# Choosing experts in smaller groups of tiles near the end of layers 0 and 2, and handing out scatters without a limit in the last steps of layer 2

## The chip, the cores and the metric

The kernel runs on one core of a Trainium2 chip. The metric is the time of one execution on the device, in microseconds (us); lower is better. The core has a matrix engine (TensorE, PE in the profile), a vector engine (VectorE, DVE), a scalar engine (ScalarE, ACT), a general engine (GpSimd, POOL) and a sync engine (SyncE, SP) that here only issues DMA transfers. Each works through its own queue in order; they wait for each other by semaphores. GpSimd also issues the indirect DMA transfers, here called scatters: 128 rows are written to 128 places in DRAM that a column of integer indices gives.

## The reference, cut to what matters

8192 tokens of 128 numbers pass through four layers, each a cross attention with 16 heads and then a feed-forward part. The feed-forward parts of layers 0, 2 and 3 are mixtures of 8 experts. Layers 0 and 2 are the ones that the change touches:

```python
# layer 0: one expert for each token, at most T / E = 1024 tokens for an expert
logits = xf @ W_sw + b_sw;  probs = softmax(logits)
routes = argmax(probs);     onehot = one_hot(routes, E)
pos = cumsum(onehot, axis=0) - 1          # place within the expert, in order of the tokens
keep = pos_tok < capacity
buf[routes, pos_safe] = xs;  expert_out = gelu(buf @ W1 + b1) @ W2 + b2
final = where(keep, expert_out[routes, pos_tok], xs)

# layer 2: the two best experts for each token, no capacity
weights, indices = top_k(softmax(x @ router), 2)
norm_weights = softmax(weights)
out = sum over the two experts e of norm_weight_e * (silu(x @ G[e]) * (x @ U[e])) @ D[e]
```

The place of a token within its expert counts all tokens before it, so groups of tokens are placed one after the other.

## The kernel before

**Tiles and groups.** The tokens are 64 tiles of 128 and stay in `x_sb` in SBUF for the whole run, 132 columns a token (128 numbers and four for the routing). While a layer's attention is still running, the experts of the tiles that are finished are chosen, group by group, and their rows are scattered to a table in DRAM (`slots`), sorted by expert. The experts' part then reads the table tile by tile. It can only begin when the last scatter has landed: every read (`xe`) waits for all scatters.

**What choosing consists of.** For a group: `variance` (seven small VectorE operations, L238 to L244), `root` (two on ScalarE, L248 and L250), `norms` (four on VectorE, L255 to L258 and L1531), `tokens` (normalised rows `fxn`: on GpSimd, L1118, in layer 0, and on ScalarE, L1552, in layer 2, where GpSimd also copies the group's rows to `rec`, L1548, since each row goes to two places), `turn` (four transposes `prt` on TensorE, L1562, and a copy `rT` on ScalarE, L1564), `logits` (four pairs of matmuls `plg`, L1571, and a move on VectorE), `offs` and `exps` (a maximum, a subtraction, an exponential), `best` (VectorE: some 19 operations in layer 2, L1600 to L1635, and six in layer 0, L1132 to L1154, that end with `took` and `before`), `gates` (layer 2) and `places` (two matmuls `pup` on TensorE, L1167 and L1168 or L1654 and L1655, and VectorE's indices: `fc_r` at L1178 in layer 0, `pl_i` at L1668 in layer 2). `places` puts one scatter for each tile (layer 0) or two (layer 2) in the list `ready`; `scatter(n)` (L1679) issues at most n of them, all from line L1683. In layer 2, `tables` (L1704) computes from the final counts which expert each tile of the table belongs to.

**Order.** A plan says in which step of the attention each of these parts is issued. TensorE's order is written by hand (`manual_schedule`) in layer 0; in layer 2 TensorE's, ScalarE's and VectorE's are. On GpSimd the scheduler may move things, but `after_scatters` (L1698) makes the first GpSimd operation that comes after some scatters in the program wait for their issue, and later scatters wait for it, so these keep the program's order.

**Layer 0** (`wide_steps`, L317) has a step for each tile, i = 0 to 64; `scatter(2)` closes every step, and what the plan has left after step 64 follows with `scatter(16)`. The groups are 16, 16, 16, 8, 4 and 4 tiles. Counted from the step at which its last tile is done, a group of 16 has its `places` nine steps on, a group of 8 six, and a group of 4 three; with 4 tiles, `logits`, `best` and `places` are all in that third step.

**Layer 2** (`head_steps`, L589, with `layer == 2`) has a step n for each two tiles, n = 0 to 31, and then up to 39 without heads; each step has two halves, h = 2n and 2n + 1, in which the plan's parts and then a `scatter` are issued: at most 3 in the first half and 2 in the second while n is below 32, later 16 and 2. Within a step TensorE's order is: the maxima of step n + 1 (`sa`), the values of step n - 1 (`pav`), a piece of a later projection, the output of step n - 2 (`py`, L992), the parts of h = 2n, the scores of step n (`sb`), `po` of step n - 1, another piece, the parts of h = 2n + 1, and a transpose of the maxima (`pm`). In every odd n, the first piece is `head_tokens` (L730): GpSimd normalises four tiles (`xn`, L741) and adds a bias to them (L748), and TensorE at once transposes the four `xn` (`pxn`, L756). The last such call is in n = 27, for tiles 60 to 63. The groups are six of 8 tiles (0 to 47) and four of 4. After a group's last tile e, `places` comes at h = e + 13 for a group of 8 that ends with tile e, at e + 10 for a group of 4, and at e + 7 for the last one, which has a shorter plan and then `tables`. So tiles 32 to 39 are placed at h = 52, tiles 40 to 47 at 60, 48 to 51 at 61, 52 to 55 at 65, 56 to 59 at 69, and 60 to 63 at 70.

Of the kernel before, what the change touches and what calls it, by code (L numbers as in the profile page):

```python
# [41 lines left out]
class Net:  # L42
# [546 lines left out]
    def head_steps(self, layer, w, NH):  # L589


        proj, mT, aT, raw, o = {}, {}, {}, {}, {}
        self.ctxT = {}
        self.context(0)

        def piece(n, late):

            g, step = (n // 2 + 1, n % 2) if layer == 3 else ((n + 3) // 2, (n + 1) % 2)
            if 4 * g >= self.NT:
                return  # L600
            if g not in proj:
                proj[g] = {}
                self.head_tokens(g, layer, w, proj[g])
            step = 2 * step + late
            if layer == 3:
                step = (0, 2, 1, 3)[step]
                if step == 1 and 4 * g + 4 < self.NT:

                    proj[g + 1] = {}
                    self.head_tokens(g + 1, layer, w, proj[g + 1])  # L610
            if step == 0:
                if layer == 2:
                    self.head_mask_read(g, proj[g])
                self.head_transpose(g, proj[g])
            elif step == 1:
                if layer == 2:
                    self.head_mask(g, proj[g])
                self.head_queries(g, w, proj[g])
            elif step == 2:
                if layer == 2:  # L620
                    self.head_mask_T(g, proj[g])
                self.head_keys(g, w, proj[g])
            else:
                self.head_new_values(g, w, proj[g])

        proj[0] = {}
        outputs = {}
        if layer != 2:
            outputs = self.outputs_plan(layer)
            for step in sorted(outputs):  # L630
                if step[0] < (-2 if layer == 3 else 0):
                    for do in outputs.pop(step):
                        do()
        self.head_tokens(0, layer, w, proj[0])
        self.head_keys(0, w, proj[0])
        self.head_new_values(0, w, proj[0])
        if layer == 2:
            self.head_mask_read(0, proj[0])
            self.head_mask(0, proj[0])
            self.head_mask_T(0, proj[0])  # L640
        self.head_transpose(0, proj[0])
        self.head_queries(0, w, proj[0])
        if layer == 3:

            first = self.first_plan(3)
            for n in range(-2, NH + 8):
                for do in outputs.pop((n, 0), ()):
                    do()  # L650
                new, old, older = (0 <= m < NH for m in (n, n - 1, n - 2))
                if new:
                    st = self.head_stable(n, proj[n // 2])
                    self.head_stable_exp(st, 0)
                if old:
                    raw = self.head_values(n - 1, aT.pop(n - 1))
                if new:
                    self.head_stable_sum(st, 0)
                    self.head_stable_exp(st, 1)
                if older:  # L660
                    oT = self.head_turn(o.pop(n - 2))
                if new:
                    piece(n, False)
                    self.head_stable_sum(st, 1)
                for do in first.pop(2 * n, ()):
                    do()
                self.scatter(2 if n < NH else 16)
                if old:
                    o[n - 1] = self.head_back(layer, raw)
                if new:  # L670
                    self.head_stable_exp(st, 2)
                if older:
                    self.head_output(n - 2, layer, w, oT)
                    if n % 2 == 1:
                        self.first_fill(2 * n - 6)
                if new:
                    self.head_stable_exp(st, 3)
                    self.head_stable_sum(st, 2)
                    piece(n, True)
                for do in first.pop(2 * n + 1, ()):  # L680
                    do()
                self.scatter(2)
                if new:
                    self.head_stable_sum(st, 3)
                    aT[n] = st["aT"]
                for do in outputs.pop((n, 1), ()):
                    do()
            return
        piece(-1, False)
        piece(-1, True)  # L690
        mT[0] = self.head_maxima_T(0, self.head_maxima(0, proj[0]))
        choice = self.choice_plan() if layer == 2 else {}
        scatter = self.scatter if layer == 2 else lambda n: None
        for n in range(NH + 8):
            for do in outputs.pop((n, 0), ()):
                do()
            if n + 1 < NH:
                mx = self.head_maxima(n + 1, proj[(n + 1) // 2])
            if 0 <= n - 1 < NH:
                raw[n - 1] = self.head_values(n - 1, aT.pop(n - 1))  # L700
            if n < NH:
                piece(n, False)
            if 0 <= n - 2 < NH:
                self.head_output(n - 2, layer, w, o.pop(n - 2))
            for do in choice.pop(2 * n, ()):
                do()
            scatter(3 if n < NH else 16)
            if n < NH:
                aT[n] = self.head_softmax(n, proj[n // 2], mT.pop(n))
            if 0 <= n - 1 < NH:  # L710
                o[n - 1] = self.head_back(layer, raw.pop(n - 1))
            if n < NH:
                piece(n, True)
            for do in choice.pop(2 * n + 1, ()):
                do()
            scatter(2)
            if n + 1 < NH:
                mT[n + 1] = self.head_maxima_T(n + 1, mx)
            if 0 <= n - 1 < NH and layer != 2:
                o[n - 1] = self.head_turn(o[n - 1])  # L720
            for do in outputs.pop((n, 1), ()):
                do()
# [331 lines left out]
    def first_plan(self, layer):  # L1054
# [3 lines left out]
        norms, tokens, turn, logits = self.choice_norms, self.first_tokens, self.choice_turn, self.choice_logits  # L1058
        offs, exps, best, places = self.choice_offs, self.choice_exps, self.first_choose, self.first_places
        at = lambda f, t0: lambda g: f(g, t0)  # L1060
        if layer == 0:
            sizes = [16] * (self.NT // 16 - 1) + [8, 4, 4]
            plans = {
                16: [
                    (1, [variance, root]), (2, [norms, at(tokens, 0), at(tokens, 4)]),
# [38 lines left out]
        plan, i0 = {}, 0  # L1104
# [354 lines left out]
    def choice_constants_from(self, whole):  # L1459

        nc, const = self.nc, self.const
        self.groups = [(i, 8) for i in range(0, self.NT - 16, 8)]
        self.groups += [(i, 4) for i in range(self.NT - 16, self.NT, 4)]
        self.go_on = {}
        for n in (4, 8, 16):
            t = const.tile([P, E, n + 1], F32, name=f"go_on{n}")
            nc.gpsimd.memset(t, 1.0)
            nc.gpsimd.memset(t[:, :, 0:1], 0.0)
            self.go_on[n] = t
        ej = whole.tile([P, E], I32, name="ej")  # L1470
        nc.gpsimd.iota(ej, pattern=[[self.T, E]], base=0, channel_multiplier=0)
        self.expert_row = const.tile([P, E], F32, name="expert_row")
        nc.vector.tensor_copy(self.expert_row, ej)
        self.last_row = const.tile([P, E], F32, name="last_row")
        nc.vector.tensor_scalar_add(self.last_row, self.expert_row, -1.0)
        jj = whole.tile([1, self.NJ], I32, name="jj")
        nc.gpsimd.iota(jj, pattern=[[1, self.NJ]], base=0, channel_multiplier=0)
        self.tile_no = const.tile([1, self.NJ], F32, name="tile_no")
        nc.vector.tensor_copy(self.tile_no, jj)
# [13 lines left out]
    def choice_plan(self):  # L1493
# [18 lines left out]
            ],  # L1512
            [
                (0, [variance, root, norms]), (1, [at(tokens, 0), at(turn, 0)]),
                (2, [at(logits, 0), offs, exps]), (3, [best]), (4, [gates, places, tables]),
            ],
        ]
        plan, last = {}, len(self.groups) - 4
        for k, (i0, n) in enumerate(self.groups):
            g = {"i": i0, "n": n, "xT": {}, "xn": {}}  # L1520
            for when, calls in ends[k == last + 3] if k >= last else long:
                when += 2 * ((i0 + n) // 2 + 1)
                plan.setdefault(when, []).extend([(lambda f=f, g=g: f(g)) for f in calls])
        return plan

    def norms_to_rows(self, g):
# [486 lines left out]
```

## Time and profile before

| | us |
|---|---|
| median of 9 runs (lowest, highest) | 2697.72 (2691.32, 2703.39) |
| the profiled execution | 2692.33 |
| its span on the core | 2690.6 |

Where the span goes, by stretches (busy time of each engine in us, and the mean TensorE clock that was granted, 1.00 being full speed):

| stretch (us from the start) | length | PE | DVE | ACT | POOL | PE clock |
|---|---|---|---|---|---|---|
| 0 to 815: layer 0, attention and choosing | 815 | 743 | 411 | 380 | 241 | 0.98 |
| 815 to 965: layer 0, experts | 150 | 125 | 35 | 56 | 70 | 0.90 |
| 965 to 1270: layer 1, attention | 305 | 259 | 201 | 157 | 55 | 0.92 |
| 1270 to 1485: layer 1, feed-forward | 215 | 111 | 177 | 150 | 131 | 0.71 |
| 1485 to 1905: layer 2, attention and choosing | 420 | 363 | 235 | 192 | 161 | 0.92 |
| 1905 to 2150: end of choosing, layer 2, experts | 245 | 206 | 159 | 145 | 159 | 0.90 |
| 2150 to 2510: layer 3, attention | 360 | 254 | 292 | 241 | 167 | 0.84 |
| 2510 to 2690: layer 3, experts | 180 | 136 | 58 | 56 | 81 | 0.86 |

The table is read by rows: an engine whose busy time is close to the length sets the pace there. The change lies at the end of the first and around the boundary of the fifth and sixth stretch. A line of a timeline has the start, the length, engine, line, operation, output and inputs, and in brackets how long the engine sat idle before it and who ended that; a merged line stands for several instructions (x4). A scatter's line shows its time on GpSimd, not the transfer.

### The profile page before, as it was taken

To read this page: it belongs to the slowest core of one execution; us is meant where nothing else is said; L and a number is where in the kernel's file an instruction comes from. 1 tells how busy PE (TensorE), PEld (TensorE's weight loads), DVE (VectorE), ACT (ScalarE), POOL (GpSimd) and SP (SyncE) were. 2 spreads that over 40 slices of the span, in tenths; PEclk is the share of its full clock that TensorE was granted. 3 is DMA by queue.
4 is the path that set the end of the run, shared out by engine and by line. 5 is a ranking of instruction groups with operands and counts; after the bars stand their busy time and mean duration, and the time that the engine had idled before them with its cause. 6 is when DMAs were issued, how large, how long until landed. Compare 5 with 4: busy or idle time off the path is not lost.

```text
span 2690.6 us, 75308 instructions
## 1 busy us (share of the span) xinstructions
PE 2196.7 (82%) x31578; PEld 1693.9 (63%) x31578; DVE 1568.7 (58%) x4342; ACT 1376.4 (51%) x2712; POOL 1063.7 (40%) x1307
## 2 busy tenths in 40 slices
PE   5999999999987968996546898988399867777597
PEld 4777777777765746775324575666299845555465
DVE  5555454554542256656887565555577668888432
ACT  3444444444433425563777454444277547777232
POOL 2222243232343551111665305533666672344444
PEclk9999999999997969998677898999599968888599
DMA  9994000000002140000000101110133450111121
GB/s 254 271 245 101 10 24 24 12 20 22 16 24 71 41 144 15 22 19 13 0 1 1 25 16 38 37 31 27 59 90 90 130 153 25 42 35 40 49 61 43
DMA packets 215363, 157.41 MB, mean 59 GB/s; under 512 B 27237, under 2 KB 191984, under 8 KB 215025
## 3 DMA queue, kind: packets, MB, share of 16 engines
q1 hardware_dynamic: 193744, 117.22, 16.9%
q0 software_dynamic: 16640, 32.22, 3.6%
q8 instruction: 250, 4.10, 0.6%
q10 hardware_dynamic: 4640, 3.15, 0.4%
q14 instruction: 89, 0.72, 0.1%
HBM read 68.62 MB, written 86.31 MB: 58 GB/s over the span
## 4 chain that ended last, share of the span: by engine, by line
PE 55%; DVE 17%; ACT 9%; POOL 9%; issue 5%; DMA 5%; SPq 0%; DVEq 0%; POOLq 0%; ACTq 0%
PE pqk L391 9%; PE ph L1817 4%; PE py L487 4%; PE pv L413 4%; PE po L473 3%; POOL slots L1683 3%; PE py L1838 2%; PE sb L879 2%; PE pav L937 2%; PE ph L1231 2%; PE sc L429 2%; PE pt L457 2%; PE pye L1250 2%; PE sb L886 2%; ACT low L920 2%
## 5 line engine op out<-in xcount | busy, mean ns | idle before, releaser
L446 POOL TENSOR_TENSOR a<-a,sm 128x1024 f32<-128x1024 f32 x64 | 121.7, 1901 | 448.6 <-DVE sm L445 231.7
L891 ACT ACTIVATE aT<-sb 128x512 f32<-128x512 f32 x256 | 132.1, 603 | 181.6 <-PE sb L886 181.6
L852 DVE TENSOR_REDUCE mpad<-sa 128x8 f32<-128x512 f32 x256 | 158.9, 683 | 95.7 <-PE sa L847 95.6
L492 DVE TENSOR_TENSOR x_sb<-x_sb,py 128x128 f32<-128x128 f32 x64 | 18.4, 288 | 287.7 <-PE py L487 287.7
L460 ACT COPY aT<-pt 128x512 f32<-128x512 f32 x128 | 68.8, 589 | 207.2 <-PE pt L457 207.2
L1683 POOL DMA_INDIRECT slots<-x_sb,fc_r x128 | 124.8, 975 | 100.1 <-DVE fc_r L1178 50.7
L1848 POOL DMA_INDIRECT outs<-ye,to x136 | 133.7, 983 | 77.6 <-DVE ye L1844 55.6
L741 POOL TENSOR_SCALAR xn<-x_sb,gn_nm,gn_r 128x128 f32<-128x128 f32 x128 | 58.0, 466 | 246.2 <-PE pxn L756 168.2
L937 PE MATMUL pav<-aT,vb 128*32 128x64 f32 x6144 | 122.5, 231 | 31.0 <-DVE aT L923 19.6
L391 PE MATMUL pqk<-xnT,L_Wq 128*128 128x256 f32 x512 | 123.0, 395 | 21.4 <-ACT xnT L383 21.4
L1817 PE MATMUL ph<-xT,gw 128*128 128x128 f32 x1088 | 133.6, 276 | 0.0
L937 PEld LDWEIGHTS pav<-aT,vb 128*32 128x32 f32 x6144 | 102.4, 116 | 49.0 <-DVE aT L923 23.2
L487 PEld LDWEIGHTS py<-L_wog,oT 128*128 128x128 f32 x1024 | 125.8, 194 | 7.4 <-DVE oT L478 4.3
L487 PE MATMUL py<-L_wog,oT 128*128 128x128 f32 x1024 | 126.7, 278 | 3.8 <-DVE oT L478 3.8
L413 PE MATMUL pv<-L_Wv,ctxT 128*64 128x512 f32 x480 | 129.5, 618 | 0.0
L1683 POOL DMA_INDIRECT slots<-x_sb,pl_i x64 | 62.0, 969 | 168.8 <-DVE r L959 136.6
L1250 PEld LDWEIGHTS pye<-L_w,hT 128*128 128x128 f32 x1024 | 119.1, 192 | 14.3 <-issue 11.5
L1817 PEld LDWEIGHTS ph<-xT,gw 128*128 128x128 f32 x1088 | 127.9, 193 | 0.2 <-ACT gw L1807 0.2
L391 PEld LDWEIGHTS pqk<-xnT,L_Wq 128*128 128x128 f32 x512 | 97.5, 195 | 41.8 <-ACT xnT L383 29.1
L1250 PE MATMUL pye<-L_w,hT 128*128 128x128 f32 x1024 | 119.2, 275 | 0.0
L1231 PE MATMUL ph<-xeT,L_w 128*128 128x512 f32 x256 | 118.2, 605 | 0.0
L473 PEld LDWEIGHTS po<-aT,v 64*64 64x64 f32 x4096 | 77.7, 136 | 63.4 <-ACT aT L460 51.5
(327 smaller groups left out, 5971.6 us busy)
## 6 DMA issues: line engine op xcount, KB each, us to landing
slots<-zero SPq DMA_DIRECT2D x80, 528.0 KB
ctxT<-in_ctxT_dram SPq DMA_DIRECT2D x63, 256.0 KB
y<-outs SPq DMA_DIRECT2D x24, 512.0 KB
xe<-slots SPq DMA_DIRECT2D x136, 66.0 KB
xe<-slots SPq DMA_DIRECT2D x32, 264.0 KB
L_w<-in_L_ffn_W_dram SPq DMA_DIRECT2D x32, 256.0 KB
outs<-fxn SPq DMA_DIRECT2D x16, 256.0 KB
out_dram<-x_sb SPq DMA_DIRECT2D x16, 256.0 KB
```

What stands on the lines that cost most here:

```text
L391: nc.tensor.matmul(ps[:, cc, :], lhsT=wt[:, (c + cc) * P : (c + cc + 1) * P], rhs=rhs, start=True, stop=True,)
L413: nc.tensor.matmul(ps[h * S : (h + 1) * S], lhsT=tok, rhs=wv[:, h], start=True, stop=True)
L473: nc.tensor.matmul(po[h][x * S : (x + 1) * S, s, tok], lhsT=v[rows, b, 2 * s + x, :], rhs=aT[rows, 2 * s + x, tok], start=True, stop=True,)
L487: nc.tensor.matmul(py, lhsT=oT[:, h, s, :], rhs=w["wog"][:, h, s, :], start=h == 0 and s == 0, stop=h == 1 and s == 3,)
L852: nc.vector.reduce_max(mpad[:, j, 0:8], sc[j].rearrange("p b c k -> p (b c) k"), axis=AX.X)
L891: exp = nc.scalar.activation(aT[:, j], sc[j], AF.Exp)
L937: nc.tensor.matmul(pav[32 * j : 32 * j + 32, b, t, :], lhsT=vb[:, 4 * (b0 + b) + j, t, :], rhs=aT[:, j, b, t, :], start=True, stop=True,)
L1231: nc.tensor.matmul(ph, lhsT=w["w1"][:, e, c * P : (c + 1) * P], rhs=x, start=True, stop=True)
L1250: nc.tensor.matmul(py[:, t, :], lhsT=h[:, c, t * P : (t + 1) * P], rhs=w["w2"][:, e, c, :], start=(c == 0), stop=(c == 3),)
L1683: put = nc.gpsimd.indirect_dma_start(out=self.scatter_dst, out_offset=bass.IndirectOffsetOnAxis(ap=row, axis=0), in_=rec, in_offset=None,)
L1817: nc.tensor.matmul(ph[:, 2 * t + c, :], lhsT=gw[j][:, t, c * P : (c + 1) * P], rhs=xT[j // 4][:, j % 4, :], start=True, stop=True,)
L1848: put = nc.gpsimd.indirect_dma_start(out=self.outs2, out_offset=bass.IndirectOffsetOnAxis(ap=to[q][:, j % 4 : j % 4 + 1], axis=0), in_=y[: ...
```

## The change

Four edits. In layer 0, tiles 32 to 63 are now grouped 8, 8, 4, 4, 4, 4 where they were 16, 8, 4, 4. In layer 2, tiles 40 to 47 become two groups of 4, and the shorter plan, which only the last group had, is also that of tiles 56 to 59; `tables` is issued after the last group's `places` as before. In layer 2, from n = 26 on, `scatter` may issue up to 16 in either half of a step.

By the rule above, `places` in layer 2 now comes at h = 52 for tiles 32 to 39 (as before), 53 for 40 to 43, 57 for 44 to 47, 61 for 48 to 51, 65 for 52 to 55, 66 for 56 to 59 and 70 for 60 to 63. In layer 0 it comes in step 46 for tiles 32 to 39, 54 for 40 to 47, 55 for 48 to 51, 59 for 52 to 55, 63 for 56 to 59 and 67 for 60 to 63 (before: 57 for 32 to 47, 62 for 48 to 55, then 63 and 67).

```diff
@@ head_steps
-            scatter(3 if n < NH else 16)
+            scatter(3 if n < NH - 6 else 16)
...
-            scatter(2)
+            scatter(2 if n < NH - 6 else 16)
@@ first_plan
         if layer == 0:
-            sizes = [16] * (self.NT // 16 - 1) + [8, 4, 4]
+            sizes = [16] * (self.NT // 16 - 2) + [8, 8, 4, 4, 4, 4]
@@ choice_constants_from
-        self.groups = [(i, 8) for i in range(0, self.NT - 16, 8)]
-        self.groups += [(i, 4) for i in range(self.NT - 16, self.NT, 4)]
+        self.groups = [(i, 8) for i in range(0, self.NT - 24, 8)]
+        self.groups += [(i, 4) for i in range(self.NT - 24, self.NT, 4)]
@@ choice_plan
-                (2, [at(logits, 0), offs, exps]), (3, [best]), (4, [gates, places, tables]),
+                (2, [at(logits, 0), offs, exps]), (3, [best]), (4, [gates, places]),
...
-        plan, last = {}, len(self.groups) - 4
+        plan, last = {}, len(self.groups) - 6
...
-            for when, calls in ends[k == last + 3] if k >= last else long:
+            for when, calls in ends[k >= last + 4] if k >= last else long:
...
+        plan[when].append(lambda: tables(g))
         return plan
```

(NH is 32 and NT is 64.)

## The prediction

> **What bounds the kernel now.** I read the chain of work that ended last, then each engine's timeline around the two places where choosing ends. By shares the matrix engine is the bound:
>
> ```profile
> PE 55%; DVE 17%; ACT 9%; POOL 9%; issue 5%; DMA 5%; SPq 0%; DVEq 0%; POOLq 0%; ACTq 0%
> ```
>
> but not at these two places. At the end of layer 0 the chain is in GpSimd's queue. From VectorE's and GpSimd's timelines:
>
> ```profile
> 805.97 0.17 DVE L1531 TENSOR_TENSOR x_sb<-gn_nm,x_sb 128x4 f32<-128x4 f32 x1
> 809.83 0.96 POOL L1683 DMA_INDIRECT slots<-x_sb,fc_r  x1 [0.30 <-issue]
> 810.83 1.72 POOL L1118 TENSOR_SCALAR fxn<-x_sb 128x128 f32<-128x128 f32 x4
> ```
>
> The last group's norms are ready at 806.14 (805.97 and 0.17), its rows `fxn` begin at 810.83, because 16 scatters of earlier groups stand ahead from 790.83 on. At the end of layer 2 GpSimd issues without a pause from 1878.39 to 1936.98, and the experts' reads follow the last one; the last line is from the sync engine's timeline:
>
> ```profile
> 1884.24 0.95 POOL L1683 DMA_INDIRECT slots<-rec,pl_i  x1 [0.31 <-issue]
> ...
> 1904.45 0.96 POOL L1683 DMA_INDIRECT slots<-rec,pl_i  x1 [0.30 <-issue]
> ...
> 1936.02 0.96 POOL L1683 DMA_INDIRECT slots<-rec,pl_i  x1 [0.30 <-issue]
> 1938.62 24.70 SPq L1774 DMA_DIRECT2D xe<-slots  x24
> ```
>
> 16 scatters take 20.21 from the first of these lines to the second: 1.263 each. A third place counts, earlier in layer 2, in n = 27, where TensorE waits for `xn`:
>
> ```profile
> 1821.99 1.02 POOL L1683 DMA_INDIRECT slots<-x_sb,pl_i  x1 [24.36 <-DVE r L959]
> ...
> 1829.06 0.45 POOL L741 TENSOR_SCALAR xn<-x_sb,nm,rstd 128x128 f32<-128x128 f32 x1
> 1829.56 1.11 PE L756 MATMUL pxn<-ident,xn 128*128 128x128 f32 x4 [5.39 <-POOL xn L741]
> ```
>
> The indices of tiles 32 to 39 come at 1821.71 (`pl_i`), five of their scatters and one copy go first, and then the last of the four `xn` of tiles 60 to 63; TensorE idles 5.39 for it, and the rest of the layer stands behind that transpose.
>
> **Layer 2, the head of the queue.** `head_tokens` of tiles 60 to 63 is called in n = 27, so it comes after whatever h = 52 and 53 issue. Before, that is 3 + 2 scatters. Now h = 52 has no limit, so all 16 of tiles 32 to 39 are ahead, and h = 53 adds the copy `rec` of tiles 44 to 47 and all 8 scatters of tiles 40 to 43. The changed program's GpSimd queue does read 16 scatters, `rec`, 8 scatters, `xn`. The first index is later by the work of tiles 40 to 43 that now lies in n = 25: transposes (0.5 of TensorE's 0.66, overlapped) and 0.65 of VectorE (a move 0.19, a maximum 0.19, a subtraction 0.19 and gaps): 1.2, between 0 if hidden and 2.0 if `plg` (0.9) is also in the way. So: first scatter 1823.2; 16 x 1.263 = 20.2; `rec` 0.62 and a gap 0.16; 8 x 1.263 = 10.1; `xn` at 1854.3 where it was 1829.06: **+25.2** (24 to 26). Those 8 wait for their own indices, which cost a `best` (3.9, from 1871.09 to 1875.0 for four tiles) and `gates` with `places` (1.95, from 1875.71) after 1822.9; they come at about 1829, well before GpSimd is there at 1844. Behind the waiting `xn` are the bias addition, the next `rec` and all later scatters on GpSimd, and behind the waiting `pxn` everything on TensorE, then the copies on ScalarE and the maxima on VectorE. What this long wait would hide is small: `best` of tiles 40 to 43, which holds TensorE some 4 in n = 26 (`pup` waits for `took`), falls into it.
>
> **Layer 2, from `xn` to the last indices.** Before, from 1829.06 to 1918.16 (end of the last `pl_i`): 89.1. The steps, one by one. n = 27: `plg` of tiles 44 to 47 comes in, +0.9. n = 28 loses `prt` and two `plg` (0.5 + 0.9 + 0.8) and gains a `pup` (0.4) on TensorE, and `best` fits VectorE's gaps (3.27 and 0.81 idle before 1850): -1.0. n = 30 took 15.9 (1860.02 to `pav` at 1875.94), because VectorE had a `best` of 8 tiles (1860.06 to 1864.5) and their `gates` and `places` (1869.2 to 1871.1) there besides the next group's; without these some 9.7, -6.2; a step without them, n = 29, took 9.1. From there on tiles 56 to 59 run on the short plan between the last heads: TensorE now waits for ScalarE's rows (1.65 for four) with `prt` of tiles 52 to 55 and of 56 to 59 in n = 31, and `best` (3.9) of both groups and `gates` lie ahead of the last residual on VectorE, where before only the one group's did. Laid out from `pav` this gives 46 to the last `pl_i` against 42.2: +3.8. Sum -2.5: 86.6, so the last indices at 1940.9. Bounds: -12 if each step takes its best (9.1 for n = 30, no waits for ScalarE), +4 if n = 30 saves nothing.
>
> **Layer 2, the end of the queue.** Before, 15 scatters start after the last index: its last starts at 1936.02, 17.9 after. Now the others are out by then (tiles 52 to 55 and 56 to 59 have indices some 22 and 15 earlier, and need 10.1 each), 8 are left: 0.3 + 7 x 1.263 = 9.1, **-8.8**. `tables` stays behind the last `pl_i` and costs nothing: its first part is written 3.1 after it (1918.0 to 1921.2), its second 8.2 after it; the 8 scatters and the landing (2.27) cover both, and with the cover gone it would cost up to 8. The last scatter thus starts at 1950.0 against 1936.02: +25.2 - 2.5 - 8.8 = **+13.9**, between +4 and +20.
>
> **Layer 0.** Only 4 scatters are left when the last group's norms are ready, and they are issued before them, so `fxn` starts at 806.2: **-4.6**; the chain behind it (`prt`, `plg`, `places`, 4 scatters) stays. Against that stand TensorE's new waits. A group of 4 has `logits`, `best` and `places` in one step, and TensorE waits for VectorE and ScalarE in between; this was so in step 63 only, now also in 55 and 59:
>
> ```profile
> 793.99 0.61 PE L1167 MATMUL pup<-took,tri 128*128 128x32 f32 x2 [1.94 <-DVE took L1150]
> ...
> 701.72 5.41 PE L391 MATMUL pqk<-xnT,L_Wq 128*128 128x256 f32 x16 [0.68 <-ACT xnT L383]
> ```
>
> Step lengths beyond the bare 11.98 and 10.85: the group of 16 at tiles 16 to 31 cost 6.6, that at 32 to 47 9.2 with a slow stretch (the second line: 5.41 against 3.72 usually, at a granted clock of 0.50 from 702 to 704), the group of 8 4.4: 13.6. New: each 8 half of 6.6 and a little, 3.6; each 4 a transposition 0.44, `plg` 0.8, the wait 1.94, `pup` 0.5: 3.7; sum 14.6, +1.0. Each new wait may bring a slow stretch of 1.7; I take one: **+2.7** (1.0 to 6). Layer 0 in sum -1.9 (-3.6 to +1.4). The row fills (256 KB, on SP) move earlier past loads of `ctxT` that are due eight steps of 12 later: covered; uncovered, a step would wait for one load.
>
> The clock decides one term here. [...] The rows differ: after the 1.94 above the grant is 0.50 at once, and at 702 it fell after gaps of only 0.78 and 0.68. [...]
>
> **Sum.** 13.9 - 1.9 = +12.0. Against the profiled execution (2692.33, of which 2690.6 is span) 2704.3; that execution lies 5.4 below the median of the nine, and against the median 2697.72 the forecast is 2709.7.
>
> **The rivals.** *Faster: the queue in n = 27 doesn't decide.* Place: GpSimd at h = 52 to 54. If `xn` were no later than before, layer 2 would gain 2.5 + 8.8, and with layer 0 the time would be 2697.7 - 13.2 = 2684.5. It decides from the point where `xn` starts before 1842.3 (12.0 earlier), with at most 14 scatters ahead. For it: GpSimd was idle for 24.36 before 1821.99 and 11.50 before 1852.37, so the scatters as such find room. Against it: the queue's order, and that indices come only at 1822. *No difference: the wait is made up.* If the 86.6 shrink to 77, layer 2 comes to +4 and the time to 2700. For it: n = 30 had VectorE work that is gone. Against it: the other steps are at 9 to 12 already without waits. *Slower still:* slow stretches after both waits in layer 0 and n = 30 saving nothing: +18 to +20, 2717.
>
> **How the numbers follow.** The measurement can tell about 0.2% (5.4) from no change. Forecast 0.66; faster rival 0.13; made up 0.13; slower still 0.08. Faster by over 0.2%: 0.13; within: 0.13; slower: 0.74. Range 2698 to 2719: from the made-up case to the slower one with the runs' own spread.
>
> **What would show it.** `xn` at about 1854 with TensorE idle some 25 in front of `pxn`; 24 scatters and a copy ahead of it; n = 30 near 10; the last scatter near 1950, alone with 7 others; in layer 0 `fxn` right behind the norms and two new waits of 1.9 at `pup`. I am wrong if `xn` comes before 1842, or if the last indices come less than 80 after it.

## The result and the profile after

| | before | after |
|---|---|---|
| median, us (lowest, highest; runs) | 2698.23 (2690.39, 2704.27; 39) | 2718.36 (2712.93, 2725.23; 12) |
| ratio after / before, 95% interval | | 1.0078 [1.0068, 1.0088] |
| the profiled execution | 2692.33 | 2720.99 |
| its span | 2690.6 | 2719.0 |

The kernel is slower by some 20 us, where 12.0 were forecast. In 14 of the 18 runs of the experiments the kernel before itself took 2865 to 2874 us, and the profiles of the edited kernels taken there show TensorE idle in gaps that the profile before doesn't have, so every ratio is taken against runs of the kernel before from the same set, and the median of these is given beside it; "with gaps" and "without gaps" name the two.

The table follows six profiled executions without gaps through the same places (us from the start of each). "Change" stands twice, since it was run once more; the last three columns are experiments told below.

| place | before | change | change, again | change, limit lifted from n = 27 | layer 0 only | old groups |
|---|---|---|---|---|---|---|
| scores of step 63, layer 0 | 782.2 | 792.8 | 790.6 | 793.1 | 789.2 | 781.3 |
| last group's norms | 806.0 | 815.5 | 810.9 | 813.3 | 812.0 | 804.1 |
| its `fxn` | 810.8 | 815.8 | 811.2 | 813.6 | 812.3 | 804.4 |
| first expert tile (`pxe`), layer 0 | 830.2 | 834.9 | 830.4 | 832.7 | 831.5 | 823.7 |
| layer 2's first matmul (`pb`, L570) | 1487.4 | 1493.1 | 1488.6 | 1491.0 | 1494.1 | 1481.5 |
| first maxima (`sa`), layer 2 | 1503.6 | 1506.2 | 1501.7 | 1507.0 | 1508.3 | 1497.7 |
| last `pl_i` | 1918.0 | 1945.2 | 1940.8 | 1926.1 | 1923.1 | 1911.0 |
| last scatter | 1936.0 | 1955.3 | 1950.9 | 1936.1 | 1941.7 | 1921.1 |
| first expert's `py`, layer 2 | 1950.7 | 1970.8 | 1966.3 | 1951.7 | 1957.2 | 1936.1 |
| layer 2, first `sa` to first `py` | 447.1 | 464.6 | 464.6 | 444.7 | 448.9 | 438.4 |
| layer 2, `pb` to first `py` | 463.3 | 477.7 | 477.7 | 460.7 | 463.1 | 454.6 |
| span | 2690.6 | 2719.0 | 2708.3 | 2700.7 | 2709.1 | 2678.1 |

Single executions of one kernel lie up to 10 us from its median, so the spans of two columns are not to be subtracted; the length of a stage says more, and medians decide.

The chain that ended last, by engine, in the changed kernel. Its line answers to the first one of the prediction:

```profile
PE 50%; DVE 19%; ACT 10%; POOL 8%; DMA 6%; issue 6%; SPq 1%; DVEq 0%; POOLq 0%; ACTq 0%
```

TensorE's share is five points lower; VectorE's is two higher, and those of ScalarE, of transfers and of "issue" one each.

Layer 0, GpSimd's timeline in the changed kernel (start, length, engine, line, operation, output and inputs, idle time before it and who ended that; line numbers behind L1523 are one higher than before):

```profile
810.43 0.96 POOL L1684 DMA_INDIRECT slots<-x_sb,fc_r  x1 [0.30 <-issue]
815.78 1.73 POOL L1118 TENSOR_SCALAR fxn<-x_sb 128x128 f32<-128x128 f32 x4 [4.39 <-DVE x_sb L1532]
```

The scatters are out at 811.39 and GpSimd waits 4.39 for the norms, where the norms waited for GpSimd before: the 4.6 came as forecast. But the norms themselves are 9.5 late (815.5 for 806.0). TensorE's timeline shows one part of why:

```profile
705.55 0.41 PE L1167 MATMUL pup<-took,tri 128*128 128x32 f32 x2 [1.84 <-DVE took L1150]
705.83 0.41 PE L1168 MATMUL pup<-before,ones 128*128 128x32 f32 x2
706.17 1.55 PE L429 MATMUL sc<-kT,qT 64*64 64x64 f32 x64
707.65 1.97 PE L413 MATMUL pv<-L_Wv,ctxT 128*64 128x512 f32 x4
```

The wait of step 55 is there (that of step 59 too, 1.84 at 757.49), and the work behind it is slow: `pv` takes 1.97, three microseconds later the same operation takes 1.08; the granted clock is 0.50 from 708 to 710. In the second execution of the change the wait of step 55 is as long (1.84 at 703.38), but the next `pv` takes 1.08.

Layer 2, GpSimd's queue in the changed kernel, from the first scatter of tiles 32 to 39 to the last one of all:

```profile
1826.39 1.02 POOL L1684 DMA_INDIRECT slots<-x_sb,pl_i  x1 [16.37 <-DVE ch_s L1601]
...
1846.35 0.63 POOL L1549 COPY rec<-x_sb 128x528 f32<-128x528 f32 x1
1847.15 0.98 POOL L1684 DMA_INDIRECT slots<-x_sb,pl_i  x1 [0.17 <-issue]
...
1856.01 0.95 POOL L1684 DMA_INDIRECT slots<-rec,pl_i  x1 [0.30 <-issue]
1857.01 0.45 POOL L741 TENSOR_SCALAR xn<-x_sb,nm,rstd 128x128 f32<-128x128 f32 x1
...
1955.33 0.97 POOL L1684 DMA_INDIRECT slots<-rec,pl_i  x1 [0.30 <-issue]
```

16 scatters, a copy, 8 scatters, and only then `xn`, at 1857.01 where it was 1829.06. TensorE's timeline, three of the groups before which it idled:

```profile
1806.30 0.65 PE L756 MATMUL pxn<-ident,xn 128*128 128x128 f32 x4 [1.87 <-POOL xn L741]
...
1829.50 0.40 PE L1655 MATMUL pup<-took,tri 128*128 128x32 f32 x2 [1.81 <-DVE took L1625]
...
1857.51 1.12 PE L756 MATMUL pxn<-ident,xn 128*128 128x128 f32 x4 [20.73 <-POOL xn L741]
```

The long wait is the forecast one. The two short ones were not in the forecast as losses: in n = 25 the copy `rec` of tiles 40 to 43 stands ahead of `xn` on GpSimd, and in n = 26 TensorE waits for their `took`.

### The profile page after: what moved, and what is told of

The parts are those of the page before. It is cut to its first block, busy times and chain, and to the rows that moved or that the text cites. A ratio compares the mean times of both kernels' runs of the same rounds, so it can differ in the third digit from the quotient of the medians.

```text
span 2719.0 us, 75419 instructions
## 1 busy us (share of the span) xinstructions
PE 2205.7 (81%) x31590; PEld 1700.2 (63%) x31590; DVE 1577.9 (58%) x4431; ACT 1378.3 (51%) x2722; POOL 1065.3 (39%) x1308
## 4 chain that ended last, share of the span: by engine, by line
PE 50%; DVE 19%; ACT 10%; POOL 8%; DMA 6%; issue 6%; SPq 1%; DVEq 0%; POOLq 0%; ACTq 0%
PE pqk L391 9%; PE py L487 4%; PE pv L413 4%; PE po L473 3%; POOL slots L1684 3%; PE sb L879 2%; PE pav L937 2%; DMA xe<-slots 2%; PE ph L1231 2%; PE sc L429 2%; PE pye L1250 2%; ACT low L920 2%; PE pt L457 2%; PE ph L1818 2%; PE sb L886 2%
## 5 line engine op out<-in xcount | busy, mean ns | idle before, releaser
L891 ACT ACTIVATE aT<-sb 128x512 f32<-128x512 f32 x256 | 132.1, 603 | 181.7 <-PE sb L886 181.7
L413 PE MATMUL pv<-L_Wv,ctxT 128*64 128x512 f32 x480 | 130.9, 624 | 0.0
L1250 PEld LDWEIGHTS pye<-L_w,hT 128*128 128x128 f32 x1024 | 119.1, 192 | 14.4 <-issue 11.5
```

The lines of the kernel that those rows point to most:

```text
L413: nc.tensor.matmul(ps[h * S : (h + 1) * S], lhsT=tok, rhs=wv[:, h], start=True, stop=True)
L891: exp = nc.scalar.activation(aT[:, j], sc[j], AF.Exp)
L1250: nc.tensor.matmul(py[:, t, :], lhsT=h[:, c, t * P : (t + 1) * P], rhs=w["w2"][:, e, c, :], start=(c == 0), stop=(c == 3),)
```

## The experiments

"The record" in the quoted expectations is the prediction above. Several kernels were run again because their first runs had gaps.

**The whole change again.** The changed kernel as it is.

> The whole change once more. The eight runs before this one were on a chip where the kernel before takes 2866 to 2874 us and TensorE idles 85 to 110 us in gaps of 0.2 to 2.5 us for which the profile names no wait; they lie where GpSimd issues more than three scatters in a row. If this run is on such a chip too: theory A (there a scatter costs TensorE about 1 us wherever it is issued, so that the wait for xn in n = 27 is hidden by these gaps): the sum of the runs of the parts, 0.15 to 0.25% slower, ratio 1.0010 to 1.0030, no wait of more than 6 us in front of pxn in n = 27. Rival B (the wait for xn comes on top): ratio 1.006 to 1.009. If it is on a chip without these gaps: 1.0078 as before.

Measured without gaps: 1.0088 [1.0069, 1.0107] (2720.47 against 2698.11). The result holds.

**Layer 0's sizes alone.**

```diff
-            sizes = [16] * (self.NT // 16 - 1) + [8, 4, 4]
+            sizes = [16] * (self.NT // 16 - 2) + [8, 8, 4, 4, 4, 4]
```

> Layer 0's new group sizes alone (16, 16, 8, 8, 4, 4, 4, 4), layer 2 as before. The record's sum gives -1.9 us (bounds -3.6 to +1.4): ratio 0.9993. A reading of the changed kernel's trace gives another number: there the attention loop of layer 0 is 10.65 us later at its end, of which 7.1 lie in steps 41 to 48, where the first group of 8 is worked in, and 4.7 to 4.9 of gain come back at fxn, so that the first expert tile starts 4.75 us later. Theory A (the loop cost is real and stays): +4.75 us, ratio 1.0018. Rival B (it is real but given back at the start of layer 2, where the two traces come within 0.93 us of each other): +0.9 us, ratio 1.0003, with the first expert tile of layer 0 still 4 to 5 us late.

> Layer 0's new group sizes alone, once more, because in the first four runs TensorE sat idle for 85 to 110 us that no wait explains (the kernel before has none of that), which can hide other waits. Where such gaps are absent: theory A, the loop's 7 to 10 us stay and fxn gives 4.7 to 5 back: +4.75 us at layer 0's first expert tile and in the total, ratio 1.0018. Rival B, late by 4 to 5 us at layer 0's experts but given back at the start of layer 2: ratio 1.0003. The record's sum: -1.9 us, 0.9993.

> Layer 0's new group sizes alone, for a chip without TensorE's unexplained gaps. Theory A (the loop's 7 to 10 us stay, fxn gives 4.7 to 5 back): +4.75 us at layer 0's first expert tile and in the total, ratio 1.0018. Rival B: as late at layer 0's experts, but given back at the start of layer 2, where the two first traces are 0.93 apart: ratio 1.0003. The record's sum: -1.9 us, 0.9993.

> Layer 0's new group sizes alone. Three executions with these sizes and without TensorE's gaps had the first expert tile of layer 0 at +4.75, +0.13 and +2.66 against the kernel before's one profile. Without the gaps (kernel before at 2698): theory A, the loop costs more than fxn gives back: +1 to +4 us, ratio 1.0004 to 1.0015; rival (the record): -1.9 us, 0.9993. With the gaps: 0.999 to 1.001, as in three runs so far.

Measured with gaps: 1.0000 [0.9991, 1.0009], 0.9986 [0.9972, 1.0000] and 1.0007 [0.9995, 1.0018] (before: 2873.72, 2866.50, 2873.46). Without gaps, the last one: **1.0034** [1.0022, 1.0046], 2706.92 against 2697.89, so +9.2 us. That is above every value expected, and it settles the sign: layer 0's edit loses. Its loop is 7.9 to 10.8 us longer in all four executions without gaps, counted from the scores of step 40 to those of step 63. Against the kernel before, by the starts of the scores:

| from step to step | change | change, again | limit from n = 27 | layer 0 only |
|---|---|---|---|---|
| 40 to 48 | +7.1 | +5.4 | +7.1 | +5.4 |
| 48 to 54 | +0.5 | +0.5 | +0.5 | +0.5 |
| 54 to 60 | +4.2 | +3.1 | +4.4 | +4.1 |
| 60 to 63 | -2.2 | -1.2 | -1.1 | -2.1 |

Between steps 40 and 48 the first group of 8 is worked in, and the kernel before has no group there beyond the `places` of the one ahead, in step 41, which both have. TensorE waits twice for VectorE's copy of the values (timeline of TensorE in the changed kernel):

```profile
524.86 1.16 PE L473 MATMUL po<-aT,v 64*64 64x64 f32 x62 [1.12 <-DVE v L415]
...
585.79 1.16 PE L473 MATMUL po<-aT,v 64*64 64x64 f32 x62 [1.03 <-DVE v L415]
```

On VectorE the first of these copies stands behind the group's variance and norms, the second behind its `best`. These 2.15 and the matmuls of the group (1.2 for `prt`, 1.9 for `plg`, 0.7 for `pup`, somewhat overlapped) account for the 5.4. In the two executions with 7.1, the other 1.7 is one slow stretch each: `pqk` takes 5.39 at 512.17 in the one and 5.33 at 585.37 in the other, where it takes 3.72 otherwise. The first of the two waits does not come from the group being small; the kernel before has it for its groups of 16 (its TensorE's timeline, step 33):

```profile
423.85 1.16 PE L473 MATMUL po<-aT,v 64*64 64x64 f32 x62 [1.22 <-DVE v L415]
```

At `pxe`, after `fxn` gave its part back, the loss is 0.2 to 4.75, and counted from step 40 it is -0.4 to 3.7, 2.0 in the mean of the four. So only some 2 of the 9.2 lie in layer 0. The rest can be looked for in stages that the edit doesn't touch. One is the experts of layer 2. VectorE's waits there, in us in total, times, and the longest; the kernel before:

```profile
DVE xn L1789 <- DMA xe<-slots: 4.6, 14, 0.6
```

and the one with layer 0's sizes alone:

```profile
DVE xn L1789 <- DMA xe<-slots: 41.3, 72, 2.3
```

In the four executions without gaps that have layer 0's new sizes these waits are 22 to 41, in the two without (the kernel before and "old groups") 4.6 and 8.1; from its first `py` to its last that stage takes 192.9 to 199.8 against 192.7 and 192.6. In the three with gaps they are 6.0 to 9.0, no more than in the other executions with gaps (4.2 to 11.0), so these waits don't always go with the sizes, and their cause is open.

The other stage is the experts of layer 3, and here the edit shows in every profile. From the first `pxe` to the last `pye` they take 132.2 to 133.8 in all seven executions with layer 0's new sizes, with gaps or without, 131.7 to 132.1 in the seven with layer 2's new groups alone, and 130.1 to 130.9 in the six with the old groups in both layers. VectorE waits longer there at a few places for a scatter to `out_dram` to land. One such place in VectorE's timeline, the kernel before and then the change:

```profile
2574.26 0.17 DVE L1213 TENSOR_SCALAR to<-xe 128x4 int32<-128x4 f32 x1 [2.14 <-DMA out_dram<-ye,to]
```

```profile
2601.13 0.17 DVE L1213 TENSOR_SCALAR to<-xe 128x4 int32<-128x4 f32 x1 [3.48 <-DMA out_dram<-ye,to]
```

Without gaps that is 2.8 us (means of four and of two executions). Why it is so is open: the code of layer 3 is the same.

**Layer 2's edits alone**, layer 0 as before.

> Layer 2's edits alone (groups of 4 from tile 40 on, the short plan for the last two, scatters without a limit from n = 26), layer 0 as before. Record: +13.9 us, ratio 1.0052. Theory (all that the traces show between the start of layer 2, +0.93, and the first expert's py, +20.05): +19.1 us, ratio 1.0071, with xn of tiles 60 to 63 behind 24 scatters and TensorE idle some 20 us before its transposes. Rival (layer 0 carries its 4.75 us to the end): +15.3 us, ratio 1.0057.

Measured with gaps: 1.0023 [1.0014, 1.0033] (before: 2873.72), a third of the loss that the theory expected. The queue is the same, with `xn` behind 24 scatters, but TensorE does not wait for it. GpSimd's timeline of this run:

```profile
1929.64 0.96 POOL L1684 DMA_INDIRECT slots<-rec,pl_i  x1 [0.30 <-issue]
1930.65 0.45 POOL L741 TENSOR_SCALAR xn<-x_sb,nm,rstd 128x128 f32<-128x128 f32 x1
```

and TensorE's:

```profile
1932.75 0.26 PE L937 MATMUL pav<-aT,vb 128*32 128x64 f32 x1 [1.84 <-issue]
...
1934.19 1.35 PE L937 MATMUL pav<-aT,vb 128*32 128x64 f32 x38 [0.45 <-issue]
1935.47 1.12 PE L756 MATMUL pxn<-ident,xn 128*128 128x128 f32 x4
```

While the scatters are issued, TensorE needs 27 us (1908.1 to 1935.5) for `pav`, work of 1.10 otherwise, and arrives at `pxn` after `xn`. So sets with gaps can't weigh this wait. By difference, without gaps: 1.0078 and 1.0088 for the whole less 1.0034 for layer 0 leave 1.0044 to 1.0054 for layer 2, 12 to 14.6 us, give or take some 5 by the intervals and if the two parts simply add, which no run tests.

**The limit lifted one step later**, with layer 0 as before.

```diff
-            scatter(3 if n < NH - 6 else 16)
+            scatter(3 if n < NH - 5 else 16)
...
-            scatter(2 if n < NH - 6 else 16)
+            scatter(2 if n < NH - 5 else 16)
```

> As the run with layer 2's edits alone, but scatters are without a limit only from n = 27 on instead of 26, so that 5 scatters and one copy stand ahead of xn in n = 27, as in the kernel before, and not 24. Theory (the queue ahead of xn is the loss, and the rest of layer 2's edits gains 2.5 + 8.8 us, less 4.7 of new waits in n = 25 and 26): xn about as early as before, 6 to 9 us faster than the kernel before, ratio 0.9967 to 0.9978. Rival (the groups of 4 and the short plan cost as much as the queue): 0 to +10 us, ratio 1.000 to 1.004.

> Layer 2's edits with the limit lifted from n = 27 on, layer 0 as before, once more for the same reason. Where TensorE has no unexplained gaps: if the 24 scatters ahead of xn are the loss, 6 to 9 us faster than before, ratio 0.9967 to 0.9978, with TensorE's wait in front of pxn in n = 27 back at some 5 to 9 us; if the groups of 4 and the short plan cost as much, 1.000 to 1.004.

> Layer 2's edits with the limit lifted only from n = 27 on, layer 0 as before, for a chip without the gaps. If the 24 scatters ahead of xn in n = 27 are the loss: xn back to within 5 us of the kernel before, 6 to 9 us faster, ratio 0.9967 to 0.9978. If the groups of 4 and the short plan cost as much as the queue: 1.000 to 1.004.

> Layer 2's edits with the limit lifted only from n = 27 on, layer 0 as before, alone with the kernel before as the run of the whole change was, which had 2698 us for the kernel before and no gaps. If the 24 scatters ahead of xn in n = 27 are the loss: xn back to within 5 us of the kernel before, 6 to 9 us faster, ratio 0.9967 to 0.9978. If the groups of 4 and the short plan cost as much as the queue: 1.000 to 1.004.

Measured, all four with gaps: 1.0022 [1.0012, 1.0032], 1.0015 [1.0004, 1.0026], 1.0018 [1.0009, 1.0027], 1.0018 [1.0006, 1.0030] (before: 2873.72, 2866.50, 2873.46, 2865.24). Within what "the groups cost as much" would give, but no verdict, for the reason just shown: with gaps the same kernel with 24 scatters ahead of `xn` (1.0023) is no slower.

**The whole change, limit lifted one step later.** The same two lines in the changed kernel.

> The whole change, layer 0's sizes too, but with the limit lifted from n = 27 on instead of 26. Without TensorE's unexplained gaps (kernel before at 2698): if the 24 scatters ahead of xn in n = 27 are the loss, TensorE's 20.7 in front of pxn fall to 3 to 9 and the time to 2692 to 2700, ratio 0.998 to 1.0007; if the groups of 4 and the short plan are, 2710 or more, ratio 1.0045 and up. With the gaps (kernel before at 2865 to 2874), where a scatter holds TensorE up wherever it stands: 1.0005 to 1.002, like the same edit with layer 0 as before (1.0018, 1.0015, 1.0022).

Measured without gaps: **1.0007** [0.9992, 1.0022], 2701.72 against 2697.51. One step of the limit is worth 0.0071, 19 us, nearly all of the loss. TensorE's timeline in n = 27:

```profile
1832.42 0.30 PE L861 MATMUL pm<-ident,mpad 128*128 128x128 f32 x1 [0.74 <-DVE ch_w L1643]
1838.44 1.12 PE L756 MATMUL pxn<-ident,xn 128*128 128x128 f32 x4 [2.72 <-POOL xn L741]
```

20.73 have become 2.72, and layer 2 (first `sa` to first `py`) is 444.7, 2.4 shorter than before. With layer 0's 9.2 taken off, layer 2's part in the median is 1.0007 less 1.0034, some 7 us of gain, give or take 5. So the gain has the sign that the theory gave; whether it is its 6 to 9 or the 2.4 of the stage is not settled.

**Only the limit lifted**, from n = 26, groups and plans as before.

> The kernel before with only the limit on scatters taken away from n = 26 on; groups and plans as before. Theory A: without the groups of 4 nothing is scattered in h = 53, so that nothing ties xn to that half step and it is ahead of the 16 scatters of tiles 32 to 39 in GpSimd's queue; TensorE's wait of 5.39 us goes and the queue's end is up to 4.4 earlier: -5 to -10 us, ratio 0.9964 to 0.998. Rival B (a lifted limit by itself puts 16 scatters before xn): 11 x 1.263 = 13.9 us later at xn, 4.4 to 9 of it regained at the end: ratio 1.002 to 1.0035.

> The kernel before with the limit lifted from n = 26 on and nothing else, once more for the same reason. Where TensorE has no unexplained gaps: with nothing scattered in h = 53, xn of tiles 60 to 63 is ahead of the 16 scatters: -5 to -10 us, ratio 0.9964 to 0.998. Rival: 16 scatters before xn, 1.002 to 1.0035.

> The kernel before with the limit lifted from n = 26 on and nothing else, for a chip without the gaps. Theory A (nothing is scattered in h = 53, so nothing ties xn to that half step; xn goes ahead of the 16 scatters): TensorE's 5.39 go and the queue's end is up to 4.4 earlier, -5 to -10 us, ratio 0.9964 to 0.998. Rival B (a lifted limit by itself holds xn up): 1.002 to 1.0035.

Measured, all with gaps: 1.0026 [1.0018, 1.0035], 1.0011 [0.9998, 1.0024], 1.0019 [1.0010, 1.0028] (before: 2873.72, 2866.50, 2873.46). The gain is missing, though `xn` does stand ahead of the 16 scatters in the queue. Not tried without gaps by itself.

**`xn` untied.** Layer 2's edits as in the change, layer 0 as before, but in `head_tokens`:

```diff
-            if layer != 1:
+            if layer == 3:
                 self.after_scatters(op)
...
-        if layer != 1:
+        if layer == 3:
             self.after_scatters(op)
```

> Layer 2's edits as in the change (limit lifted from n = 26, groups of 4, short plan), layer 0 as before, but in layers 0 to 2 head_tokens' xn and bias addition are no longer ordered behind scatters on GpSimd; only rec still is. Theory (the tie of xn to the scatters of the half step before is the whole loss): TensorE's wait in n = 27 goes (20.7 in the changed kernel) and so do the waits of some 5.4 in the other odd steps (26.8 in all in layer 2 before): 20 to 35 us faster than before, ratio 0.987 to 0.9925. Rival (the waits move to the next thing, such as the maxima on VectorE): 0.995 to 1.000.

> Layer 2's edits with the limit lifted from n = 26 as in the change, layer 0 as before, but head_tokens' xn and bias addition no longer ordered behind scatters, for a chip without the gaps. Theory (the order that ties xn to the scatters is the whole loss, here and, by 5.4 at a time, in the other odd steps, 26.8 in all): 20 to 35 us faster than before, ratio 0.987 to 0.9925. Rival (the waits move to the next late thing): 0.995 to 1.000.

Measured, both with gaps: 1.0031 [1.0018, 1.0044] and 1.0051 [1.0038, 1.0065] (before: 2866.50, 2873.46). A miss, slower even than the rival expected. Whether untying gains without gaps wasn't tried.

**The old groups with the other edits.** The kernel before, with the limit lifted from n = 26, the short plan for the last two groups of layer 2 (`tables` after the last group, as in the change), and in layer 0 more scatters in the last steps in place of smaller groups:

```diff
-            self.scatter(2)
+            self.scatter(2 if i < 60 else 5)
...
-            scatter(3 if n < NH else 16)
+            scatter(3 if n < NH - 6 else 16)
...
-            scatter(2)
+            scatter(2 if n < NH - 6 else 16)
...
-            for when, calls in ends[k == last + 3] if k >= last else long:
+            for when, calls in ends[k >= last + 2] if k >= last else long:
```

> The kernel before with three edits, groups in both layers as before: in layer 2 the limit on scatters lifted from n = 26 and the short plan also for tiles 56 to 59 (tables after the last group); in layer 0 scatter(5) instead of scatter(2) from step 60 on. Layer 0 and layer 2 are read apart, by the start of layer 0's first expert tile and by layer 2's stages. Without TensorE's unexplained gaps: layer 0: fxn of the last group right behind its norms, no new waits in the loop, 3 to 4.6 us earlier. Layer 2: nothing is scattered in h = 53, so xn of tiles 60 to 63 is ahead of the 16 scatters and TensorE's 5.39 go; no work of tiles 40 to 43 in n = 25 to 27, so the 7.5 us go that these steps cost in the last run; 8 scatters instead of 16 after the last index, 8 us. Sum -13 to -20, ratio 0.9926 to 0.995. Rival (the runs of 16 scatters hold up rec and the indices instead): 0.997 to 1.001. With the gaps: 0.999 to 1.003.

> The same kernel as the run before (old groups; limit lifted from n = 26 and short plan for the last two groups in layer 2; five scatters a step from step 60 in layer 0), which fell where TensorE has its unexplained gaps (kernel before at 2865; ratio 1.0035). If these gaps are absent here (kernel before at 2698): -13 to -20 us, ratio 0.9926 to 0.995, with the last group's fxn in layer 0 right behind its norms and TensorE without a wait in front of pxn in n = 27; rival 0.997 to 1.001. If they are there: 1.002 to 1.005 again.

Measured with gaps 1.0035 [1.0020, 1.0050] (before: 2865.03); without gaps **0.9943** [0.9930, 0.9957], 2680.59 against 2697.40. This version beats both kernels there. Layer 0, from GpSimd's timeline:

```profile
799.04 0.96 POOL L1684 DMA_INDIRECT slots<-x_sb,fc_r  x1 [0.30 <-issue]
804.38 1.73 POOL L1118 TENSOR_SCALAR fxn<-x_sb 128x128 f32<-128x128 f32 x4 [4.38 <-DVE x_sb L1532]
```

`fxn` is right behind the norms, as in the change, without a longer loop (step 63 at 781.3 for 782.2): the first expert tile is 6.5 earlier. Some 1.1 of this is chance: the loop of this execution lacks the slow stretch that the kernel before has at 701.72. Layer 2, from GpSimd's and then TensorE's timeline:

```profile
1791.89 1.27 POOL L748 TENSOR_TENSOR x_sb<-x_sb,add 128x512 f32<-128x512 f32 x1
1815.71 1.02 POOL L1684 DMA_INDIRECT slots<-x_sb,pl_i  x1 [22.56 <-DVE r L959]
```

```profile
1817.81 0.65 PE L756 MATMUL pxn<-ident,xn 128*128 128x128 f32 x4
```

`xn` and its bias addition were done at 1793, 22 us before the first of the 16 scatters, because with groups of 8 nothing is scattered in h = 53 and so no order ties them to it. The wait of 5.39 in front of `pxn` is gone, 10.1 lie between the last `pl_i` and the last scatter instead of 18.0, and layer 2 is 8.7 shorter. So neither gain needed the smaller groups.

## Why the prediction was right or wrong

The direction was right, and in layer 2 the place and the mechanism; the size was 12.0 against some 20. By the medians 9.2 are layer 0's, where -1.9 was forecast, and 12 to 14.6 layer 2's, where it was +13.9. What failed is layer 0.

*The queue in n = 27: right.* `xn` is 27.95 later, and layer 2 was late already: counted from its first `sa` it is 25.4, from the `pxn` of n = 23, the last ahead of the new work, 26.5; forecast +25.2. TensorE idled 20.7 in front of `pxn` and not some 25, since n = 25 to 27 had become longer before it came there.

*From `xn` to the last index: -0.7 (88.2 against 88.9), forecast -2.5.* n = 30 took 10.2 (forecast 9.7, before 15.9), and what follows it 45.5 (46, before 42.1). The 1.8 are missing in n = 27 to 29, which took 1.6 longer where 0.1 less was forecast. The work ahead of the wait was underestimated too, but in the change the wait hides that: in the run with the limit lifted later, TensorE needs 6.8 us more than before from the scores of n = 24 to those of n = 27, though its wait for `xn` there is 2.7 shorter, because `rec`, `lg` and `took` of the additional group are waited for in n = 25 and 26. The forecast had 1.2 for that work beside the `best` that it held hidden.

*The end of the queue: right.* 10.1 from the last `pl_i` to the last scatter instead of 18.0, -7.9 for -8.8; one scatter took 1.55. `tables` stayed covered: from the last scatter to `py` 15.5 after 14.7.

*Layer 2 in sum:* +13.9 forecast, 12 to 14.6 by the medians. By the stage it depends on where the counting begins: +14.5 and +14.4 in the two executions of the change from `pb`, +17.5 from the first `sa`, +19.2 and +19.1 from the `pxn` of n = 1. Between these places both gained 4.7 on the kernel before, whose matmuls run slowly for longer there (its first `sa`, from `off`, takes 1.91, that of the change 1.03). That is chance of an execution: the edits don't touch it, and the run with layer 0's sizes alone gained 2.1 there. From `pb` that run has -0.2, from `sa` +1.8.

*Layer 0's loop: wrong, and this is the step that failed.* The 4.6 at `fxn` came. The term "+2.7 (1.0 to 6)" for the loop measured 7.9 to 10.8 in four executions up to the scores of step 63, and 4.4 to 8.5 up to the last group's norms, since the last two steps got shorter. It was made by halving: "each 8 half of 6.6 and a little, 3.6". The 6.6 were too small: by the scores' starts in the kernel before, steps 33 to 43 together are 7.9 longer than bare ones, and the 1.35 in step 33 that are not in the 6.6 are the wait of 1.22 for `v` behind the variance and the norms. And this part doesn't shrink: the wait is 1.12 for a group of 8. VectorE's small operations ahead of that copy, seven for the variance and two of the four for the norms, take 0.17 to 0.19 each for a group of 16 and 0.16 to 0.17 for one of 8, and they are paid for each group; six groups became eight. So the first group of 8 cost 5.4, and the second saved nothing against the group of 16 that the kernel before works in at the same steps (+0.5 from step 48 to 54). The two waits for `took` were foreseen, and each came at 1.84 or 1.85.

And the loss did not stay in layer 0: of the 9.2 some 2 are there at `pxe`. The forecast had no term for later stages. Four executions with the new sizes against the two without give 3.9 more in the experts of layer 2 and 2.8 in those of layer 3, in sum 8.7 with the 2.0; that is an estimate from single executions. The 2.8 go with the edit, the 3.9 are not shown to, and the cause of both is open.

*The clock:* the slow stretches came, and more often than the forecast took. In the changed kernel the grant is 0.68 from 706 to 708 and 0.50 from 708 to 710, behind a wait of 1.84. Of the eight such waits (1.84 or 1.85) in the four executions with the new sizes and without gaps, seven were followed by a slow stretch (the next `pv` takes 1.46 to 1.97, otherwise 1.08), where the forecast took one of two, and one was not, after the same 1.84: the length of the wait alone doesn't decide it.

*The rivals:* the faster one needed `xn` before 1842.3; with one step of the limit changed it came at 1837.93, and layer 2 did turn to a gain. The case "made up" did not occur. The slower still one was right in its first half, both slow stretches, but not in its second, n = 30 saving nothing; that the time came out near its 2717 is luck.

## What to carry to other kernels

A limit on how much a queue may take at once also protects what stands behind it: before lifting it, look for the next thing in that queue that the busy engine waits for, and lift it just after that; here one step made 19 of 20 us. Smaller groups, which shortened the tail of layer 2 from 18.0 to 10.1, pay only if what each group costs regardless of its size (in layer 0 the wait for `v`, 1.12 with 8 tiles and 1.22 with 16) is hidden; the short plan and more scatters a step gave the same 10.1 with the old groups. And a gain that comes from moving work past a queue should be tried on its own, without the regrouping that came with it.

## What the runs showed of the hardware

In 14 runs TensorE idled in short gaps for which the profile names nothing (85 to 110 us an execution in the first four of them, the longest single one 5.1), and the kernel before took 2865 to 2874 us; in 4 runs, and in the profile at the beginning, there were almost none (0.3 at most). The gaps are not all of the 170 us; the mean granted clock was 0.88 to 0.89 with them and 0.90 to 0.91 without. The chip alone does not decide it: on the one that the record numbers 13 the kernel before took 2698.11 in one set of runs and 2873.46 in another. In the two stretches of timeline shown here the gaps lie where GpSimd issues scatters back to back: the 27 us of `pav` in the run with layer 2's edits alone, and step 26 of layer 0 in the first run with only the limit lifted, while GpSimd issues six scatters from 339.60 to 347.14. TensorE's timeline of the latter:

```profile
341.94 1.53 PE L473 MATMUL po<-aT,v 64*64 64x64 f32 x48
343.88 0.35 PE L473 MATMUL po<-aT,v 64*64 64x64 f32 x4 [0.41 <-issue]
344.62 0.30 PE L473 MATMUL po<-aT,v 64*64 64x64 f32 x3 [0.39 <-issue]
345.37 0.36 PE L473 MATMUL po<-aT,v 64*64 64x64 f32 x6 [0.45 <-issue]
346.83 0.34 PE L473 MATMUL po<-aT,v 64*64 64x64 f32 x3 [1.10 <-issue]
```

Three to six matmuls, then nothing; the step took 19.5 instead of 12.2. The step after it, with two scatters, kept its length (10.85, as in the kernel before). What TensorE waits for in the gaps no run here shows. The comparison has a use all the same: with gaps the best version here is 0.35% slower and without them 0.57% faster, so an edit that bundles scatters has to be judged in both.
